# A state-space block on one core: the table request moved into the scan, two thirds of a convolution moved to VectorE, y sums one slot earlier, decay weights made later

## The chip, the cores and the metric

The kernel runs on one core of a Trainium2 chip. A core has TensorE (PE: matmuls; its weight loads are counted apart as PEld), VectorE (DVE), ScalarE (ACT), GpSimd (POOL) and SyncE (SP), which here issues all the transfers. Each engine works through its own queue in order and waits on semaphores. The metric is the device time of one launch in microseconds (us), the median of several runs.

## The reference

The input x has 8 images of 96 channels with 64 x 64 pixels. Layer 0 is a group norm (groups of three channels) and a vision state-space block, with a residual. Layer 1 is an attention without softmax and a small feed-forward net in a coarse float format, both with residuals. What matters here is the block:

```
xh      = layernorm(groupnorm(x))
xi, z   = split(xh @ in_proj_w.T + in_proj_b)        # 192 channels each
xi      = silu(depthwise 3x3 conv(xi) + conv_b)
xs      = xi in 4 orders of its 4096 pixels          # rows, columns, both reversed
dts,B,C = xs @ x_proj_w                              # per order
delta   = softplus(dts @ dt_proj_w + bias)
h[t]    = exp(delta[t] * A) * h[t-1] + delta[t] * xs[t] * B[t]   # 16 states per channel
y[t]    = sum over states of h[t] * C[t]  +  D * xs[t]
out     = x + (layernorm(sum of the 4 y) * silu(z)) @ out_proj_w.T + b
```

A is -exp(A_log), a constant. Every sum is in fp32, but for the feed-forward net.

## The kernel before, in words

The images are worked off in four pairs, each through five stages.

**front** (L217) normalizes both images chunk by chunk (8 chunks of 512 pixels; L261 to L270), projects them (L276 to L303) and convolves. The projected channels lie in three padded images `ybuf`: T = 0 and 1 hold channels 0 to 127 of the first and second image, T = 2 the last 64 of both (64 partitions each). The depthwise convolution is nine matmuls per chunk with a diagonal weight matrix `diag` (L311), added up in PSUM; ACT applies Silu on the way out into `xi[T]` (L316). The diagonals are made by DVE at the start of each front, 18 of them (L226).

**prepare** (L329) makes delta, delta times input, B and C from `xi` and writes them to device memory in the layout of the scan. It ends with a request for the table set `LOGEXP`, in which ACT has both logarithm and exponential (L397). ACT evaluates a function only with a table set that contains it; where the set in force lacks the function, the compiler puts in a load.

**scan** (L400) goes over 4 orders x 32 time chunks = 128 steps. A step has eight slots v. In slot v, for p = 8s + v: PE multiplies delta by A for slot p + 2 and ACT takes exp in place (`decay`, L533 and L537); POOL makes delta u B for two slots at a time (`drive`, L515); DVE runs the recurrence over 774 columns (`run`, L548) from `da[p % 3]` and `dbu` into `h`; and PE sums the states of the step before with C as the weights (`sums`, L566), two of the sixteen positions of each block per group f, eight groups in all. After the groups 3 and 7 ACT takes the sums out of PSUM (`yev`, L574). `da` has three buffers, `dbu` three, `h` two. So the first `run` of step s + 1 writes the buffer of h that the groups of step s - 1 read, and these are worked off during step s. This part is written in a hand-made order (`manual_schedule`): each engine takes the instructions as the program has them.

**back** (L628) adds up the four orders through PE, normalizes (ln and exp, L698 and L699), gates and projects. **tail** (L717) does layer 1: a first part with a norm and the key and value products per chunk, a second with the feed-forward net; `norm` has a logarithm at L735 and an exponential at L736.

Outside the scan a planner orders the instructions on each engine: it simulates the program with costs of its own, takes what is ready, and prefers what comes first in the program. Pools that are closed give their space to pools opened after them, and a tile waits until the tiles that had its space have been read.

Before all this, constants are loaded, and the weights that multiply delta by A are made: exp of A_log, three bf16 parts of it, written to device memory (`ad`), read back spread over partitions, multiplied with a mask by DVE (`awp`, L179) and written out again (`awd`, 1.5 MB for each of the four orders). The scan loads them at L429, first at its own start.

Of the kernel before, what the change touches and what calls it, by code (L numbers as in the profile page):

```python
# [10 lines left out]
F32 = mybir.dt.float32  # L11
F16 = mybir.dt.float16
BF16 = mybir.dt.bfloat16
F8 = mybir.dt.float8e5
AF = mybir.ActivationFunctionType
ALU = mybir.AluOpType
# [4 lines left out]
DI = 192  # L21
NS = 16
RK = 6
KD = 4
HH = 64
L = HH * HH
F = 512
NCH = L // F
ROWS = F // HH
# [9 lines left out]
NE = 24  # L39
X0 = F - 3 * SEG  # L40
LOGEXP = "natural_log_exp_and_others"
# [10 lines left out]
def vss_attn_ffn(ctx: ExitStack, tc: tile.TileContext, a: dict):  # L52
    nc = tc.nc
# [13 lines left out]
    ident = const.tile([128, 128], F32, name="ident")  # L67
# [13 lines left out]
    for e in range(4):  # L81
        rows = slice(NE * e, NE * e + NE)
# [9 lines left out]
    convw = load("convw", [128, 2, 9])  # L92
    convb = load("convb", [128, 2])
# [5 lines left out]
    with tc.tile_pool(name="xprep", bufs=2) as wp:  # L99
        for k in range(KD):  # L100
            for g in range(2):
                xg = wp.tile([128, 3, 2 * NS], F32, name="xg")
                nc.sync.dma_start(xg, a["xw"][k, :, g, :, 0:32])
                for b in range(2):
                    o = 32 * g + NS * b
# [31 lines left out]
    for g in range(2):  # L137
        for e in range(4):
# [1 line left out]
                dpad[:, g, 32 * e : 32 * e + NE], ident[0:DIM, NE * e : NE * e + NE],  # L140
                dsum[:, g : g + 1], None, ALU.mult,
            )

    ad = dram.tile([3, KD, DI, NS], BF16, name="ad", bufs=1)
    awd = dram.tile([KD, 128, 48 * 128], BF16, name="awd", bufs=1)
    with tc.tile_pool(name="aprep", bufs=1) as wp:
        am = wp.tile([128, KD, 2, NS], F32, name="am")  # L150
        nc.sync.dma_start(am, a["alog"])
        nc.scalar.activation(am, am, AF.Exp)
        nc.vector.tensor_scalar(am, am, -1.0, None, ALU.mult)
        for i in range(3):
            ap = wp.tile([128, KD, 2, NS], BF16, name=f"ap{i}")
            nc.vector.tensor_copy(ap, am)
            if i < 2:
                nc.vector.tensor_tensor(am, am, ap, ALU.subtract)
            for k in range(KD):
                nc.sync.dma_start(ad[i, k, 0:128], ap[:, k, 0])  # L160
                nc.sync.dma_start(ad[i, k, 128:DI], ap[0:64, k, 1])
        mask = wp.tile([128, 16], F32, name="mask")
        for p in range(3):
            nc.sync.dma_start(
                mask[32 * p : 32 * p + 32],
                ident[0:16, 0:16].unsqueeze(1).to_broadcast([16, 2, 16]),
            )
        for p in range(2):
            nc.sync.dma_start(mask[96 + 16 * p : 112 + 16 * p], ident[0:16, 0:16])
        for k in range(KD):  # L170
            ac = wp.tile([128, NE * NS], BF16, name="ac", bufs=2)
            for i, rows, n in ((0, slice(0, 96, 2), 6), (1, slice(1, 96, 2), 6), (2, slice(96, 128), 4)):
                nc.sync.dma_start(
                    ac[rows],
                    ad[i, k].rearrange("(s c) n -> s (c n)", s=8).unsqueeze(0)
                    .to_broadcast([n, 8, NE * NS]),
                )
            aw = wp.tile([128, 48, 16, 8], BF16, name="awp", bufs=2)
            nc.vector.tensor_tensor(  # L179
                aw,  # L180
                ac.rearrange("p (c n) -> p c n", n=8).unsqueeze(2).to_broadcast([128, 48, 16, 8]),
                mask.unsqueeze(1).unsqueeze(3).to_broadcast([128, 48, 16, 8]), ALU.mult,
            )
            nc.sync.dma_start(awd[k], aw.rearrange("p c m n -> p (c m n)"))


    blk = const.tile([128, 16], F32, name="blk")
    nc.sync.dma_start(blk, ident[0:16, 0:16].unsqueeze(1).to_broadcast([16, 8, 16]))
# [24 lines left out]
    def half(T):  # L213
        return 1 if T == 2 else 0


    def front(pair, xi, zs, ybuf):  # L217
        with ExitStack() as st:
            p1 = st.enter_context(tc.tile_pool(name="p1", bufs=1))
            tmp = st.enter_context(tc.tile_pool(name="p1t", bufs=2))  # L220
            ps = st.enter_context(tc.tile_pool(name="p1ps", bufs=4, space=PSUM))

            diag = p1.tile([128, 2, 9, 128], F32, name="diag")
            for j in range(2):
                for t in range(9):
                    nc.vector.tensor_scalar(  # L226
                        diag[:, j, t, :], ident, convw[:, j, t : t + 1], None, ALU.mult
                    )
            pad = [t.rearrange("p (h w) -> p h w", w=HH + 2) for t in ybuf]
            for t in ybuf:  # L230
                nc.gpsimd.memset(t, 0.0)
# [38 lines left out]
                    nc.vector.tensor_scalar(xt[:, cs], xt[:, cs], nw, nb, ALU.mult, ALU.add)  # L270


            for b in range(2):
                xt = xts[b]
                lo = slice(64 * b, 64 * b + 64)
                for c in range(NCH):  # L276
                    cs = bass.ts(c, F)
                    r0 = c * ROWS
                    pm = ps.tile([128, F], F32, name="pm", tag="ps")
                    nc.tensor.matmul(pm, winT[:, 0:128], xt[:, cs], start=True, stop=True)  # L280
                    pl = ps.tile([128, F], F32, name="pl", tag="ps")
                    nc.tensor.matmul(pl[lo], winT[:, 128:DI], xt[:, cs], start=True, stop=True)
                    nc.scalar.activation(
                        pad[b][:, r0 + 1 : r0 + 1 + ROWS, 1 : HH + 1],
                        pm.rearrange("p (h w) -> p h w", w=HH),
                        AF.Identity, bias=inb[:, 0:1],
                    )
                    nc.scalar.activation(
                        pad[2][lo, r0 + 1 : r0 + 1 + ROWS, 1 : HH + 1],
                        pl[lo].rearrange("p (h w) -> p h w", w=HH),  # L290
                        AF.Identity, bias=inb[lo, 1:2],
                    )
                    zt = tmp.tile([DIM, 2, F], F32, name="zt")
                    for g in range(2):
                        pz = ps.tile([128, F], F32, name="pz", tag="ps")
                        nc.tensor.matmul(
                            pz[:DIM], winT[:, DI + g * DIM : DI + (g + 1) * DIM], xt[:, cs],
                            start=True, stop=True,
                        )
                        nc.scalar.activation(  # L300
                            zt[:, g], pz[:DIM], AF.Silu, bias=inz[:, g]
                        )
                    nc.sync.dma_start(zs[b, :, :, cs].rearrange("g p l -> p g l"), zt)  # L303

            for T in range(3):
                for c in range(NCH):
                    r0 = c * ROWS
                    pc = ps.tile([128, F], F32, name="pc", tag="ps")
                    for t in range(9):
                        dy, dx = divmod(t, 3)  # L310
                        nc.tensor.matmul(  # L311
                            pc, diag[:, half(T), t, :],
                            pad[T][:, r0 + dy : r0 + dy + ROWS, dx : dx + HH],
                            start=(t == 0), stop=(t == 8),
                        )
                    nc.scalar.activation(  # L316
                        xi[T][:, bass.ts(c, F)], pc, AF.Silu, bias=convb[:, half(T) : half(T) + 1]
                    )

    def spread(dst, T, src):  # L320

# [7 lines left out]
    def prepare(xi, us, dl, du, bs, cs_):  # L329
        with ExitStack() as st:  # L330
# [8 lines left out]
            for o in range(2):  # L339
                for c in range(NCH):  # L340
# [12 lines left out]
                    for k in (o, o + 2):  # L353
# [12 lines left out]
                        for T in range(3):  # L366
# [27 lines left out]
                                .rearrange("j a p t -> p (j a) t"),  # L394
                                T, dp.rearrange("p j a t -> p (j a) t"),
                            )
            nc.scalar.preload_act_table_set(LOGEXP)  # L397


    def scan(dl, du, bs, cs_, ys):  # L400
        with ExitStack() as st:
            st.enter_context(tc.manual_schedule())
            one = st.enter_context(tc.tile_pool(name="s1", bufs=1))
            wk = st.enter_context(tc.tile_pool(name="s2", bufs=2))
            trio = st.enter_context(tc.tile_pool(name="s3", bufs=3))
# [196 lines left out]
            for s in range(N + 2):  # L602
                for v in range(8):
                    p = 8 * s + v
                    if s < N:
                        decay(p + 2)
                        if v % 2 == 0:
                            drive(p // 2 + 2)
                        run(p)
                    if 0 < s <= N:  # L610
                        sums(s - 1, v)
                    if s < N:
                        if v == 0:
                            load(s + 1)
                        if v == 1:
                            fetch(2 * s + 3)
                        if v == 5:
                            fetch(2 * s + 4)
                        if s + 1 < N and steps[s + 1][2] and v % 2 == 1:
                            load_aw(steps[s + 1][0], v // 2)  # L620
                    if v == 3 and s > 1:
                        store(s - 2)
                    if v == 0:
                        more = diagonal(s + 1) if s % NB else load_bc(s + NB)
                    next(more, None)
# [197 lines left out]
    for pair in range(npair):  # L823
# [7 lines left out]
        with tc.tile_pool(name="xip", bufs=1) as xp:  # L831
            xi = [xp.tile([128, L], F32, name=f"xi{T}") for T in range(3)]
            with tc.tile_pool(name="yp", bufs=1) as yp:

                ybuf = [yp.tile([128, (HH + 2) ** 2], F32, name=f"y{T}") for T in range(3)]
                front(pair, xi, zs, ybuf)
            prepare(xi, us, dl, du, bs, cs_)
        scan(dl, du, bs, cs_, ys)
        with tc.tile_pool(name="t1p", bufs=1) as tp:
# [117 lines left out]
```

## Time and profile before

| | |
|---|---|
| time, median of 3 runs | 13196.79 us (13184.92 to 13217.89) |
| profiled execution | 13189.4 us |
| PE busy | 9569.7 us (73%) |
| DVE busy | 8359.3 us (63%) |
| POOL busy | 7825.5 us (59%) |
| ACT busy | 7498.9 us (57%) |
| DMA | 2043.74 MB, 155 GB/s over the span |

The stages of the second pair, by the first and last instruction of their lines in the trace: norm of the front from 3374.9 us, projection from 3465, convolution 3529.5 to 3715, preparation to about 4057, scan to 5970, back end to 6280, tail to about 6615. The busy shares are means over these stages. A group of instructions has its line, engine, operation, output and inputs, count, busy time, the mean of one in ns, and the idle time of its engine just before it with what ended most of that. "issue" as a releaser means that the engine waited for nothing that the profile shows.

### The profile page before, as it was taken

What the parts mean: (1) busy time and instruction counts of PE and PEld (TensorE: products, weight loads), DVE (VectorE), ACT (ScalarE), POOL (GpSimd) and SP (SyncE); (2) the same over time, 40 slices, a digit from 0 to 9 for tenths busy, and PEclk for the clock granted to TensorE, in tenths of its full rate; (3) what the DMA queues carried; (4) which work ended last, traced back from release to release, by engine and by line L of the source; (5) the groups of instructions that cost most, each with busy time, mean ns of one, the idle gap of its engine ahead of it and who ended that gap; (6) DMA issues with size and microseconds to landing.
All of it is one profiled execution on the core that took longest, in us unless ns stands there. A gap on an engine that the chain in (4) does not pass through costs nothing. (4 is left out here: it accounts for less than half of the span.)

```text
span 13189.4 us, 405730 instructions
## 1 busy us (share of the span) xinstructions
PE 9569.7 (73%) x179456; PEld 6167.3 (47%) x179456; DVE 8359.3 (63%) x6293; ACT 7498.9 (57%) x12586; POOL 7825.5 (59%) x2686
## 2 busy tenths in 40 slices
PE   7966666687796666668779566666868956666686
PEld 2245555553224555555322455555533245555553
DVE  2378988932137999992213799899221389999822
ACT  2456666635445666663544666666254566666625
POOL 0379999910037999990003799999000389999900
PEclk9778888896777888889677788888967688888896
DMA  2788888861178888886017888888601888888860
GB/s 60 158 198 197 198 196 199 197 139 23 38 160 200 198 199 204 200 200 138 9 37 178 199 202 196 197 202 196 128 11 41 177 201 200 197 200 202 188 127 10
DMA packets 1627316, 2043.74 MB, mean 155 GB/s; under 512 B 958083, under 2 KB 1303252, under 8 KB 1622740
## 3 DMA queue, kind: packets, MB, share of 16 engines
q1 hardware_dynamic: 1625556, 2017.78, 66.8%
q8 instruction: 1408, 23.07, 0.8%
q14 instruction: 352, 2.88, 0.1%
HBM read 1579.00 MB, written 438.38 MB: 153 GB/s over the span
## 5 line engine op out<-in xcount | busy, mean ns | idle before, releaser
L515 POOL TENSOR_TENSOR dbu<-dut,bc 128x1536 f32<-128x1536 f32 x2048 | 7083.1, 3506 | 602.9 <-ACT dbu L512 516.2
L548 DVE TENSOR_TENSOR_SCAN h<-da,dbu 128x774 f32<-128x774 f32 x4096 | 6973.8, 1756 | 732.9 <-ACT da L537 419.2
L537 ACT ACTIVATE da<-da 128x768 f32<-128x768 f32 x4096 | 3263.9, 797 | 2210.4 <-PE da L533 2161.8
L566 PE MATMUL yp<-h,cw 128*32 128x48 f32 x131072 | 3172.0, 242 | 925.7 <-issue 911.4
L533 PE MATMUL da<-dm,aw 128*128 128x128 bf16 x24576 | 2424.9, 244 | 1736.8 <-DVE h L548 1384.4
L566 PEld LDWEIGHTS yp<-h,cw 128*32 128x32 f32 x131072 | 2534.7, 153 | 1519.2 <-issue 1191.2
L533 PEld LDWEIGHTS <-aw 128*128 128x128 bf16 x24576 | 1825.1, 108 | 1994.5 <-issue 1649.4
L469 ACT ACTIVATE cw<-bc,blk 128x512 f32<-128x512 f32 x2048 | 1478.3, 723 | 268.0 <-DMA bc<-cs 240.4
L348 POOL COPY u<-xi 128x512 f32<-128x512 f32 x96 | 110.1, 1160 | 1517.7 <-PE pc L311 1486.8
L391 POOL TENSOR_TENSOR dp<-rest,dp 128x512 bf16<-128x512 f32 x384 | 458.4, 1194 | 713.6 <-ACT dp L390 701.2
L742 POOL MEMSET tn<- 1x4096 f32 x8 | 27.8, 3506 | 1311.4 <-DVE t L712 1311.4
L376 DVE TENSOR_TENSOR du<-delta,xi 128x512 f32<-128x512 f32 x192 | 133.0, 692 | 1060.9 <-ACT delta L372 772.5
L812 POOL TENSOR_TENSOR ot<-t,y 96x512 f32<-96x512 f32 x64 | 73.5, 1148 | 1176.2 <-DVE y L810 1150.2
L311 PE MATMUL pc<-y,diag 128*128 128x512 f32 x1728 | 742.3, 592 | 0.0
L389 DVE TENSOR_TENSOR rest<-delta,dp 128x512 f32<-128x512 f32 x384 | 303.9, 792 | 662.7 <-ACT dp L388 662.7
L368 PE MATMUL pq<-S,dtw 12*128 12x512 f32 x768 | 582.2, 866 | 122.7 <-ACT delta L372 75.3
L574 ACT ACTIVATE yev<-yp 128x384 f32<-128x384 f32 x1024 | 500.0, 488 | 198.5 <-PE yp L566 185.4
L674 PEld LDWEIGHTS py<-ident,yk 128*24 128x24 f32 x16384 | 449.3, 103 | 177.9 <-issue 176.6
L674 PE MATMUL py<-ident,yk 128*24 128x128 f32 x16384 | 509.8, 275 | 23.9 <-issue 23.5
L311 PEld LDWEIGHTS pc<-y,diag 128*128 128x128 f32 x1728 | 326.4, 189 | 415.4 <-issue 415.4
L316 ACT ACTIVATE xi<-pc,c_convb 128x512 f32<-128x512 f32 x96 | 66.0, 687 | 675.8 <-PE pc L311 675.8
L681 ACT ACTIVATE yt<-py 128x512 f32<-128x512 f32 x64 | 38.2, 597 | 721.0 <-PE py L674 670.7
(133 smaller groups left out, 7591.7 us busy)
## 6 DMA issues: line engine op xcount, KB each, us to landing
dut<-du SPq DMA_DIRECT2D x1024, 768.0 KB
dm<-dl SPq DMA_DIRECT2D x512, 576.0 KB
dl<-dp SPq DMA_DIRECT2D x256, 384.0 KB
dm<-dl SPq DMA_DIRECT2D x512, 192.0 KB
ys<-yev SPq DMA_DIRECT2D x1024, 96.0 KB
du<-du SPq DMA_DIRECT2D x256, 256.0 KB
bc<-bs SPq DMA_DIRECT2D x512, 128.0 KB
bc<-cs SPq DMA_DIRECT2D x512, 128.0 KB
```

The costliest lines, as they stand in the source:

```text
L311: nc.tensor.matmul(pc, diag[:, half(T), t, :], pad[T][:, r0 + dy : r0 + dy + ROWS, dx : dx + HH], start=(t == 0), stop=(t == 8),)
L368: nc.tensor.matmul(pq, dtw[64:76, k, T], S[64:76], start=True, stop=True)
L389: nc.vector.tensor_tensor(rest, d, dp[:, :, 0], ALU.subtract)
L391: nc.gpsimd.tensor_tensor(dp[:, :, 2], rest, dp[:, :, 1], ALU.subtract)
L469: nc.scalar.activation(cw[i % 2][:, :, :, m, :].rearrange("p z j t -> p (z j) t"), bc[i][:, 1].rearrange("p z (j t) -> p (z j) t", j=NB), ...
L515: nc.gpsimd.tensor_tensor(segs(t)[:, :, :, 1:], dut[g // 2][:, NI * (r % 2) : NI * (r % 2) + NI, :].unsqueeze(1) .to_broadcast([128, 2, NI ...
L533: nc.tensor.matmul(e[:, i], aw[k, r][:, i, z, :], dm[s][:, NI * r + i, :], start=True, stop=True,)
L537: nc.scalar.activation(e, e, AF.Exp)
L548: nc.vector.tensor_tensor_scan(hs[s][:, w, r][:, d], da[p % 3][:, o : o + W6][:, d], dbu[4 * s + r][:, w][:, d], 0.0, ALU.mult, ALU.add,)
L566: nc.tensor.matmul(y[32 * q : 32 * q + 32, 2 * NE * i : 2 * NE * i + 2 * NE] .rearrange("p (j r i) -> p i j r", j=2, r=NR), w[:, z, :, t], ...
L574: nc.scalar.activation(yev[s][:, :, o : o + 8, :].rearrange("p j i e -> p i j e"), y[:, 0 : 16 * NE].rearrange("p (i j e) -> p i j e", j=2 ...
L674: nc.tensor.matmul(o, yk[:, k, 4 * g + e, NE * j : NE * j + NE], ident, start=False, stop=(k + j == KD + 2),)
```

## The change

Four edits, each for a reason of its own:

- **Table request.** The request for `LOGEXP` leaves the end of `prepare`, where the planner places it, and becomes the first instruction of `scan`, where the written order holds.
- **Convolution.** Only T = 1 stays on PE. T = 0 and T = 2 become nine multiply-add passes on DVE over whole images (`taps`), with Silu in place on ACT behind them. T = 0 is traced after the projection of the first image, T = 2 after both. `diag` keeps nine diagonals.
- **y sums.** The groups 0 and 1 go into slot 0, each later group into one slot earlier, and slot 7 has none. This is meant to free the buffer of h before the next step needs it.
- **Weights for delta A.** The code becomes a function, called once, behind the front of the first pair, so that the constants' way to the first pair is shorter.

```
-    with tc.tile_pool(name="aprep", bufs=1) as wp:
...
+    def decay_weights():
+        with tc.tile_pool(name="aprep", bufs=1) as wp:
...
...
-            diag = p1.tile([128, 2, 9, 128], F32, name="diag")
-            for j in range(2):
-                for t in range(9):
-                    nc.vector.tensor_scalar(
-                        diag[:, j, t, :], ident, convw[:, j, t : t + 1], None, ALU.mult
-                    )
+            diag = p1.tile([128, 9, 128], F32, name="diag")
+            for t in range(9):
+                nc.vector.tensor_scalar(
+                    diag[:, t, :], ident, convw[:, 0, t : t + 1], None, ALU.mult
+                )
...
+            def taps(T):
+                for t in range(9):
+                    dy, dx = divmod(t, 3)
+                    w = convw[:, half(T), t : t + 1]
+                    v = pad[T][:, dy : dy + HH, dx : dx + HH]
+                    o = xi[T].rearrange("p (h w) -> p h w", w=HH)
+                    if t == 0:
+                        nc.vector.tensor_scalar(o, v, w, None, ALU.mult)
+                    else:
+                        nc.vector.scalar_tensor_tensor(o, v, w, o, ALU.mult, ALU.add)
+                for c in range(NCH):
+                    xc = xi[T][:, bass.ts(c, F)]
+                    nc.scalar.activation(
+                        xc, xc, AF.Silu, bias=convb[:, half(T) : half(T) + 1]
+                    )
...
+                if b == 0:
+                    taps(0)
+            taps(2)
-            for T in range(3):
-                for c in range(NCH):
+            for c in range(NCH):
...
-            nc.scalar.preload_act_table_set(LOGEXP)       # end of prepare
...
             st.enter_context(tc.manual_schedule())        # start of scan
+            nc.scalar.preload_act_table_set(LOGEXP)
...
                     if 0 < s <= N:
-                        sums(s - 1, v)
+                        for f in ((0, 1), (2,), (3,), (4,), (5,), (6,), (7,), ())[v]:
+                            sums(s - 1, f)
...
                 front(pair, xi, zs, ybuf)
+            if pair == 0:
+                decay_weights()
             prepare(xi, us, dl, du, bs, cs_)
```

## Prediction

> **What bounds the kernel now.** I read the table of time by stage first. It gives span, PE, weight loads, DVE, ACT and POOL busy (with counts), granted clock, DMA share and GB/s; the second pair of images is shown, stage by stage.
>
> ```profile
> 3380.00:3470.00 90.00, 60.87 (x69) 16.00 (x68) 23.29 (x38) 72.00 (x85) 0.00 (x0) 0.50 0.00 0
> 3470.00:3530.00 60.00, 60.00 (x126) 18.45 (x125) 0.00 (x0) 43.31 (x63) 0.00 (x0) 0.97 0.33 99
> 3530.00:3715.00 185.00, 185.00 (x432) 81.13 (x430) 0.00 (x0) 16.16 (x24) 0.00 (x0) 1.00 0.06 25
> 3834.00:4057.00 223.00, 157.94 (x213) 40.23 (x212) 105.00 (x130) 118.19 (x203) 102.47 (x83) 0.64 0.96 214
> 4057.00:5966.00 1909.00, 1291.27 (x38554) 1080.81 (x38555) 1737.56 (x1021) 1276.89 (x2285) 1770.58 (x527) 0.86 0.85 198
> 5966.00:6280.00 314.00, 275.24 (x4761) 165.83 (x4761) 68.56 (x95) 87.86 (x111) 1.39 (x1) 0.97 0.68 134
> 6280.00:6420.00 140.00, 100.97 (x346) 65.36 (x345) 17.19 (x30) 90.11 (x118) 6.95 (x2) 0.78 0.00 1
> ```
>
> These are layer norm, input projection, convolution, preparation, scan, back end and the first part of the tail. Each has another limit. The convolution is PE alone: 185 of 185 us, and DVE does nothing. Preparation is full of DMA (0.96). The scan is DVE and POOL together.
>
> Next, groups by line (busy, mean ns of one, idle before and who ended it), then what the scan instruction waited for in the first pair (us, times), then ACT's groups that load a table.
>
> ```profile
> L316 ACT ACTIVATE xi<-pc,c_convb 128x512 f32<-128x512 f32 x96 | 66.0, 687 | 675.8 <-PE pc L311 675.8
> L548 DVE TENSOR_TENSOR_SCAN h<-da,dbu 128x774 f32<-128x774 f32 x4096 | 6973.8, 1756 | 732.9 <-ACT da L537 419.2
> ```
>
> ```profile
>   ACT da L537: 116.4, 64
>   PE yp L566: 66.3, 39
>   POOL dbu L515: 6.9, 33
> ```
>
> ```profile
> L735 ACT ACT_TABLE_LOAD x128 | 164.2, 1283 | 2.3
> L736 ACT ACT_TABLE_LOAD x128 | 164.2, 1283 | 2.3
> L698 ACT ACT_TABLE_LOAD x64 | 82.1, 1283 | 1.2
> L699 ACT ACT_TABLE_LOAD x64 | 82.1, 1283 | 1.2
> L267 ACT ACT_TABLE_LOAD x48 | 61.6, 1283 | 0.9
> L268 ACT ACT_TABLE_LOAD x48 | 61.6, 1283 | 0.9
> L537 ACT ACT_TABLE_LOAD x4 | 5.1, 1283 | 0.1
> ```
>
> The reader is to see three things. The convolution's ACT waits 675.8 us for PE. The scan's 1756 ns x 1024 = 1798 us per pair are a floor, and of the idle time above it 66 us ends with the y sums on PE. And every logarithm and every exponential of back end and tail loads a table. The old request at L397 appears nowhere in the trace, while L537, the scan's exponential, loads a set itself in each pair: the request has no effect today.
>
> **What the Trainium skill says.** *ScalarE: Activation LUTs*, "Table sets: the hidden batching unit": one set holds both functions, so ln then exp needs one load. The trace agrees: L267 and L268 run 16 times each in the first pair with no load (48, not 64), after the request at L66. The same page, "What ACT_TABLE_LOAD costs", gives 1283 ns plus a drain of 1380. The trace shows 1283, but the exponential begins 0.01 us behind it, so I take 1.28 us. *VectorE: DVE Perf Modes*, "The perf-mode tier table": fp32 tensor_scalar reaches 2x, tensor_tensor 1x. The trace agrees for the first (4096 elements in 2.40 us, L256); it has no row for scalar_tensor_tensor.
>
> **Convolution.** Today 24 chunks at 7.725 us (start to start of the ACT rows at L316) = 185 us. Halves T = 0 and 2 leave PE; T = 1 keeps 8 x 7.725 = 62 us. One tap on DVE, from L706 (512 elements, all in SBUF, 740 ns) and 1 cycle an element: about 740 + 3584 x 1.04 ns = 4.5 us. Nine taps: eight at 4.5 plus a first at 2.4 to 4.5, so 38 to 40 us per half. Lower bound, if these ops ran at the 2x of L256: 22 us; upper, if the rows of 64 break the stream: 55. I take 40. Projection of the first image ends some 32 us after the stage's start, of the second 61 us. Half 0 then runs on DVE from 32 to 72, half 2 from 72 to 112, its eight Silu passes (0.69 us) to 118. The PE convolution runs from 61 to 123 and still ends last, by 5 us; it hides both halves. Gain 123 us a pair. What is queued behind the new wait: the Silu of half 0 stands in ACT's queue near the evacuations of the second image's projection, and if it is placed too early, those and PE wait for DVE. I deduct 5 us a pair for that: 118 x 4 = 472 us. Preparation begins earlier as a whole; its DMA limit moves with it.
>
> **The diagonals** halve from 18 to 9. From the second pair on they stand before the statistics in DVE's order (14.35 us for 18), so 7.2 x 3 = 22 us.
>
> **Table request.** Put in the scan's own hand-ordered program it is fixed ahead of the exponential, which is in the set; square, copy, ln and exp of back end, tail and the next front then load nothing, until Silu. Removed: 440 loads in L735/736, L698/699 and L267/268, plus 12 in L254/255, together 580 us of ACT. On the path is less: the load before ln mostly lies beside the matmul that ln waits for; the one before exp does not.
> - Norm in the front: 5.22 us a chunk in pairs 2 to 4 against 4.41 in the first. 0.81 x 16 x 3 = 39, plus about 9 for the single statistics: 48 us.
> - Last part of the tail: a period of 12.14 us in which PE waits 2.15 us for tq; 1.3 x 16 x 4 = 83 us.
> - First part: 14 us per round with four loads, ACT 91 of 140 us, PE 101. PE becomes the limit at 12 us or so: 2.3 x 8 x 4 = 75 us.
> - Back end: 18.09 us per round, PE waits 1.25 us for g; 1.23 x 16 x 4 = 79 us.
> Sum 285 us (180 to 350).
>
> **y sums one slot ahead.** Slot 0 gets two groups, slot 7 none. Today the last group stands behind decay matmuls that wait for the scan of slot 6, and h has two buffers, so the first scan of the next step waits for it. The wait of 66 us (67, 53, 52 in the others) should go. Most of it comes from PE pauses of 2.5 to 4.7 us with no releaser in the trace ("issue"), about one in 30 us. Those remain, but with the group 1.75 us earlier and decay two scans ahead, a 2.6 us pause is hidden and a 3.5 us one costs about 1.5 us. I let 70% of 238 us go: 170 us (60 to 240). The double slot adds 0.7 us to PE before the next decay, which has about 1.7 us to spare (3.5 us of lookahead less 0.5 us matmuls, 0.8 us exp and two handovers). POOL, 3.505 us per two scans, is as fast as DVE and not the limit.
>
> **Weights for delta A.** At the front of the first pair they hold the load of x until 53 us, and four DVE products of 6.5 us stand among the statistics: normalization starts at 83.7 us. Without them x is asked for near 33 us, behind the constants that the queue has issued by 30; 12 us to arrive (53.4 to 65.1 today), 5 for eight statistics, 4 for the small steps: about 54, so 30 us are won. Behind the front they take space that the padded inputs had and that preparation's tiles take next, so preparation waits for their chain: two products after the convolution's end, each with a 1.5 MB store behind it, about 30 us. I take 0, with -30 to +35.
>
> **Sum.** 472 + 22 + 285 + 170 + 0 = 949; 13197 - 949 = **12,250 us**.
>
> **Rivals.**
> - *The request is void again.* For: it was so at L397, and nothing shows why. Against: at L66 it worked, and the scan keeps its written order. 12,250 + 285 = 12,535.
> - *DVE becomes the front's bound.* Taps of 6 us, or ACT's queue held by them, halve the gain: 12,250 + 236 = 12,486. For: half 2 ends only 5 us before PE.
> - *The scan wins nothing:* each PE pause moves to "ACT da", already 419 us in all. 12,420.
> - *Slower.* The double slot puts 0.7 us on the path of each of 512 steps (358 us), DVE takes as long as PE did, the request is void: 13,197 + 358 - 22 = 13,533. Against: PE waits for DVE 0.5 to 0.7 us in nearly every slot, so it has the room.
>
> **How the numbers follow.** Forecast 0.60, void request 0.10, DVE bound 0.14, scan nothing 0.12, slower 0.04. The best ends of all terms give about 12,060; the first and second rival end at 12,535 and 12,486. Range 12,040 to 12,540. Faster 0.95, same 0.01, slower 0.04.
>
> **What would show it.** PE convolution time per pair 62 us with DVE at 80 us beside it; no table loads at L735/736 and their like; "PE yp" gone from the scan's waits and scan spans near 1,865 us; normalization starting near 54 us in the first pair. Wrong it would be if taps took over 5 us each, if ACT waits for them inside the projection, if loads stay, or if "ACT da" grows by what "PE yp" loses.

## The result, and the profile after

The changed kernel takes **12690.28 us** (median of 4 runs, 12684.31 to 12694.4), against 13197.52 for the kernel before (4 runs). The ratio is 0.9614 (95% interval 0.9597 to 0.9631): 507 us are won. The forecast was 12,250, so 440 us of the expected 949 are missing. A time below that stands without a ratio is that of one launch.

First the table of time by stage, for the second pair: stretch, its length, then PE, weight loads, DVE, ACT, POOL busy (with counts), granted clock, DMA share, GB/s. The rows are norm, projection, convolution, preparation, scan.

```profile
3241.60:3333.00 91.40, 61.53 (x69) 16.65 (x70) 26.17 (x43) 71.02 (x82) 0.00 (x0) 0.50 0.00 0
3333.00:3396.00 63.00, 63.00 (x129) 18.88 (x128) 26.93 (x9) 46.33 (x67) 0.00 (x0) 0.94 0.32 94
3396.00:3458.00 62.00, 61.95 (x145) 26.98 (x143) 50.23 (x12) 15.31 (x25) 0.00 (x0) 1.00 0.18 57
3458.00:3829.00 371.00, 288.58 (x402) 75.08 (x403) 149.40 (x198) 196.87 (x333) 157.11 (x127) 0.64 0.91 204
3829.20:5735.30 1906.10, 1309.66 (x38638) 1092.90 (x38637) 1754.38 (x1024) 1258.56 (x2277) 1764.25 (x523) 0.82 0.85 197
```

The convolution is 62 us instead of 185, and still PE's: 61.95 of 62. DVE works through projection and convolution, 27 and 50 us, and the convolution still ends with PE. The norm (91 us; 90 before) and the scan (1906; 1909) are as they were.

Next, groups by line: ACT's Silu behind the PE convolution, DVE's taps, DVE's scan.

```profile
L335 ACT ACTIVATE xi<-pc,c_convb 128x512 f32<-128x512 f32 x32 | 21.9, 685 | 173.2 <-PE pc L331 173.2
...
L283 DVE SCALAR_TENSOR_TENSOR xi<-y,c_convw,xi 128x4096 f32<-128x4096 f32 x64 | 285.2, 4482 | 1.4
...
L565 DVE TENSOR_TENSOR_SCAN h<-da,dbu 128x774 f32<-128x774 f32 x4096 | 7027.2, 1760 | 641.5 <-ACT da L554 503.2 <-PE yp L583 39.3 <-ACT dbu L529 31.6
```

Then what the scan instruction waited for in the first pair (us, times).

```profile
  ACT da L554: 125.1, 65
  PE yp L583: 9.5, 5
  ACT dbu L529: 8.0, 9
  POOL dbu L532: 3.7, 20
```

The wait on the y sums is nearly gone, 66 to 9.5 us, and the wait on delta A has grown by 9. Over all pairs "PE yp" falls from 239 to 39 us, in these lines of before and after, and "ACT da" rises from 419 to 503.

```profile
  PE yp L566: 238.6, 158
...
  PE yp L583: 39.3, 21
```

The scan's idle time falls from 733 only to 642, and of these 91 us only 37 come off the span of the scans: the busy time of the scan instructions has grown by 53, from 6973.8 to 7027.2 us. Why it has grown is open.

Last, ACT's table loads.

```profile
L753 ACT ACT_TABLE_LOAD x128 | 164.2, 1283 | 2.3
...
L716 ACT ACT_TABLE_LOAD x64 | 82.1, 1283 | 1.1
...
L267 ACT ACT_TABLE_LOAD x48 | 61.6, 1283 | 0.8
...
L554 ACT ACT_TABLE_LOAD x4 | 5.1, 1283 | 0.1
```

They are the loads of before, and one more in the setup. The request, now at L419, appears nowhere, and the scan's exponential at L554 still loads a set in each pair.

The profiled executions (13189.4 and 12691.4 us, 498 apart) give this balance, by the first and last starts of each stage's instructions:

| stage | won, us |
|---|---|
| convolution, 4 x (186.3 - 62.7) | 494 |
| first pair until its convolution (237.5 to 200.0) | 37 |
| preparation of the first pair (356.6 to 409.5) | -53 |
| preparation of the others (356.5, 357, 364.5 to 370.5, 355.2, 368.1) | -16 |
| scans (1919.7, 1897.3, 1903.8, 1908.3 to 1896.8, 1906.1, 1893.6, 1895.1) | 37 |
| sum | 499 |

Back end, tail and norm together changed by about 1 us. The other edits and the scatter of the stages sum to nearly nothing: the time is that of the convolution alone. Small terms are not to be trusted to the last microsecond. Over the traces of this case the later preparations take 351 to 378 us and the projections 64 to 79, whatever the kernel, so the -16, and 7 of the 37 before the first convolution, may be chance.

### The profile page after: what moved, and what is told of

It reads as the page before. It is cut to its first block, busy times and chain, and to the rows that moved or that the text cites. A ratio compares the mean times of both kernels' runs of the same rounds, so it can differ in the third digit from the quotient of the medians.

```text
span 12691.4 us, 403490 instructions
## 1 busy us (share of the span) xinstructions
PE 9112.9 (72%) x178304; PEld 5967.4 (47%) x178304; DVE 8711.4 (69%) x6329; ACT 7451.3 (59%) x12587; POOL 7833.1 (62%) x2686
## 3 DMA queue, kind: packets, MB, share of 16 engines
q8 instruction: 1399, 22.92, 0.9%
## 5 line engine op out<-in xcount | busy, mean ns | idle before, releaser
L565 DVE TENSOR_TENSOR_SCAN h<-da,dbu 128x774 f32<-128x774 f32 x4096 | 7027.2, 1760 | 641.5 <-ACT da L554 503.2
L554 ACT ACTIVATE da<-da 128x768 f32<-128x768 f32 x4096 | 3258.1, 798 | 2132.6 <-PE da L550 2098.6
L583 PE MATMUL yp<-h,cw 128*32 128x48 f32 x131072 | 3127.9, 245 | 1059.9 <-issue 1045.2
L550 PE MATMUL da<-dm,aw 128*128 128x128 bf16 x24576 | 2486.4, 250 | 1534.3 <-DVE h L565 1162.5
L721 DVE SCALAR_TENSOR_TENSOR g<-yc,c_onw,yrs 96x512 f32<-96x512 f32 x128 | 89.9, 742 | 556.6 <-ACT yrs L717 556.6
L385 PEld LDWEIGHTS pq<-S,dtw 12*128 12x128 f32 x768 | 160.4, 250 | 610.8 <-ACT delta L389 176.0
L407 ACT ACTIVATE dp<-rest 128x512 bf16<-128x512 f32 x384 | 241.4, 630 | 326.4 <-DVE rest L406 326.4
L529 ACT COPY dbu<-h 128x12 f32<-128x12 f32 x1984 | 407.7, 205 | 0.0
```

What stands on the lines that cost most here:

```text
L385: nc.tensor.matmul(pq, dtw[64:76, k, T], S[64:76], start=True, stop=True)
L529: nc.scalar.copy(start, segs(hs[s - 1][:, :, r])[:, :, :, 1 if back else TC])
L550: nc.tensor.matmul(e[:, i], aw[k, r][:, i, z, :], dm[s][:, NI * r + i, :], start=True, stop=True,)
L554: nc.scalar.activation(e, e, AF.Exp)
L565: nc.vector.tensor_tensor_scan(hs[s][:, w, r][:, d], da[p % 3][:, o : o + W6][:, d], dbu[4 * s + r][:, w][:, d], 0.0, ALU.mult, ALU.add,)
L583: nc.tensor.matmul(y[32 * q : 32 * q + 32, 2 * NE * i : 2 * NE * i + 2 * NE] .rearrange("p (j r i) -> p i j r", j=2, r=NR), w[:, z, :, t], ...
```

## The experiments

The theory after the result had three parts: the convolution's gain is all there is; the request is void because something replaces its set before the scan's exponential; and the y sums won little because PE's pauses without releaser hit another wait. The rival to the first was that several small gains had been cancelled by as many losses.

### Each edit undone

**convolution_on_PE** takes the changed kernel and puts 18 diagonals and three PE halves back, with the order of before:

```
-            diag = p1.tile([128, 9, 128], F32, name="diag")
+            diag = p1.tile([128, 2, 9, 128], F32, name="diag")
...
-                if b == 0:
-                    taps(0)
-            taps(2)
-            for c in range(NCH):
+            for T in range(3):
+                for c in range(NCH):
```

> The changed kernel with all three convolutions on PE again, in the old place. Theory: each pair loses the 123.6 us that the trace shows, 494 us in all: about 13,184 us. Rival: the preparation behind it is bound by DMA, which gives part of it back: under 13,080 us.

Measured: 13218.28 us, ratio to the kernel before 1.0007 (0.9995 to 1.002). With the other three edits and without this one there is no gain left that can be measured. The edit is worth 528 us by the medians, 494 by the trace. The theory's 13,184 was 34 us too low; the rival's bound of 13,080 is far off.

**sums_as_before** puts each group of y sums back into its own slot:

```
-                        for f in ((0, 1), (2,), (3,), (4,), (5,), (6,), (7,), ())[v]:
-                            sums(s - 1, f)
+                        sums(s - 1, v)
```

> The changed kernel with the y sums in their old slots. Theory: the edit traded the wait for the sums for a wait for the decay, and is worth some 37 us (the sum of the four scan spans): about 12,727 us. The forecast's size, 170 us, would give 12,860 us. Rival: the double slot costs as much as the early end brings: 12,690 us.

Measured: 12751.13 us, ratio 0.9669 (0.9638 to 0.97). The edit is worth 61 us by the medians and 50 by the spans of the scans (7642 against 7592 us), above the theory's 37 and far below the forecast's 170. The scan again waits for "PE yp", 273 us, and less for "ACT da", 410: the two waits trade places. The size stays rough, since one trace a kernel is little: convolution_on_PE has the early sums too, and its scans add up to 7641 us, as many as here.

**weights_at_the_front** makes the weights for delta A before the first front again. It is not the old place: there they stood ahead of the constants of the feed-forward net, here behind them.

```
+    decay_weights()
+
     def front(pair, xi, zs, ybuf):
...
-            if pair == 0:
-                decay_weights()
```

> The changed kernel with the weights for delta A made ahead of the first front again. Theory: behind the front they win 30 us of start and lose 53 us at the head of the first preparation, whose first copy waits 52.3 us for the last store; undone, the time falls by 23 us to about 12,667 us. The forecast had 0: 12,690 us. Rival: the start's 30 us count and the wait was hidden: 12,720 us.

Measured: 12665.75 us, ratio 0.9601 (0.9566 to 0.9636). By the medians the move costs 24 us, as expected; the interval overlaps that of the changed kernel, so the time alone does not settle it. The way there was not the expected one. In this trace x is asked for at 33.8 us and normalization starts at 54.7, as in the changed kernel (33.5 and 53.4), so the early start isn't lost here; the norm of the first pair takes 89 us instead of 75, the first preparation 356 instead of 410, and the first scan starts at 634.8 us instead of 672.3. So the old place, ahead of those constants, was not tried again, and what the move brought is known from the balance alone. The waits in the first preparation of the changed kernel show the cost directly (who waited for whom: us in total, times, longest).

```profile
POOL u L365 <- DMA awd<-awp: 305.6, 1, 305.6
...
ACT S L377 <- DMA awd<-awp: 52.3, 1, 52.3
```

Preparation's first tile `S` lies where the weights lay and waits 52 us until they are written out. (POOL's 305 us are mostly time in which it had nothing to do.) That is the 53 us by which the first preparation grew; the earlier start gives back 37.

### Where the request goes

**pin_request** leaves everything but the place of the request. It goes from the head of the scan's program behind the first of the ACT copies of C, which waits for data:

```
-            nc.scalar.preload_act_table_set(LOGEXP)
             one = st.enter_context(tc.tile_pool(name="s1", bufs=1))
...
-            for _ in diagonal(0):
+            todo = diagonal(0)
+            next(todo)
+            nc.scalar.preload_act_table_set(LOGEXP)
+            for _ in todo:
                 pass
```

> The changed kernel with the table request behind the first copy that builds C's weights in the scan, instead of at the scan's head. Theory: at the head the request waits for nothing, so the planner sets it ahead of the preparation's last Softplus, whose own load replaces it; behind an instruction that waits it stays. Then the 456 loads before ln, exp and the statistics go, 14 loads are left, and the time falls by the 285 us of the forecast, to about 12,405 us. Rival 1: a request inside the scan is dropped wherever it stands: loads as they are, 12,690 us. Rival 2: the loads go, but they lay beside other work: loads gone and over 12,600 us.

Measured: **12344.37 us**, ratio 0.935 (0.9307 to 0.9393), 346 us under the changed kernel. ACT's table loads are now these, and two single ones in the setup.

```profile
L317 ACT ACT_TABLE_LOAD x4 | 5.1, 1283 | 0.1
L389 ACT ACT_TABLE_LOAD x4 | 5.1, 1283 | 0.1
L612 ACT ACT_TABLE_LOAD x4 | 5.1, 1283 | 0.0
```

L317 and L389 are Silu and Softplus, L612 is the request: for the first time it stands in the trace, once per pair, and 492 loads have gone. From the last scan instruction of a pair to the first matmul of the next norm it is now 593.4, 594.1 and 596.5 us instead of 672.5, 679.6 and 677.0, and from the last scan instruction of all to the end 570 instead of 645. The norms of the later pairs take 74.6 us instead of 89.6. In sum 245 + 75 + 3 x 15 = 365 us, a little more than the medians give. (The four launches lie between 12,279 and 12,376 us, and the profiled one was the fastest.) The size in the forecast (285) was low; the mechanism holds as soon as the request stays.

The reading of why it did not stay: the written order holds among the scan's own instructions. A request at their head waits for nothing, so nothing keeps it behind preparation's Softplus at L389, whose own load then replaces the set. Behind a copy that waits for the scan's first data it can't go ahead. The traces show both ends of this (no load and no effect in one place, four loads and full effect in the other); a request that was passed over leaves no record, so the step between, who set it ahead and when, is inferred.

### What holds the scan

In the trace of the changed kernel, PE stops between matmuls of one group. This is the timeline: start, length, instruction, and in brackets the idle time before it and who ended it.

```profile
4263.44 0.39 PE L583 MATMUL yp<-h,cw 128*32 128x48 f32 x6 [2.52 <-issue]
...
4263.76 0.83 PE L550 MATMUL da<-dm,aw 128*128 128x128 bf16 x6
...
4264.62 0.80 ACT L554 ACTIVATE da<-da 128x768 f32<-128x768 f32 x1 [3.02 <-PE da L550]
...
4265.52 1.77 DVE L565 TENSOR_TENSOR_SCAN h<-da,dbu 128x774 f32<-128x774 f32 x1 [2.10 <-ACT da L554]
```

PE idles 2.52 us for no reason in the profile, six matmuls before the end of a group. The matmuls of delta A come behind it, then the exponential, and the scan loses 2.10 us. With the sums one slot ahead the pause no longer delays the buffer of h, but it still delays the next `decay`, which has only the 1.7 us to spare that the prediction worked out. Between 4300 and 5020 us there are 41 such pauses over 1 us, 104 us in all. The line of the y sums has the total, 1045 us of "issue" ahead of them:

```profile
L583 PE MATMUL yp<-h,cw 128*32 128x48 f32 x131072 | 3127.9, 245 | 1059.9 <-issue 1045.2
```

How much of "ACT da" comes from there can be counted in the trace. Of its 503 us, 368 come right behind such a pause (the exponential waits for PE, and a pause over 0.5 us ended at most 2.5 us before), and 118 behind a copy of C that holds ACT because its load is late.

**double_group_late** asks whether the double slot costs something where it stands. It moves it to slot 6:

```
-                        for f in ((0, 1), (2,), (3,), (4,), (5,), (6,), (7,), ())[v]:
+                        for f in ((0,), (1,), (2,), (3,), (4,), (5,), (6, 7), ())[v]:
```

> The changed kernel with the two groups together in slot 6 instead of slot 0; slot 7 stays empty. Theory (pauses set the waits, not the double slot): the time stays at 12,690 us within 20. Rival (the double slot in front of the next decay is what makes it late): at least 60 us away from it, down if slot 0 was the wrong place.

Measured: 12742.59 us, ratio 0.9654 (0.9615 to 0.9694), 52 us above the changed kernel, more than the theory's 20 and less than the rival's 60; the intervals overlap. "PE yp" returns to 178 us and "ACT da" stays at 473. The early double slot isn't the brake: moved away from the head of the step, it brings nothing.

**no_delta_loads** leaves out all but three of a scan's 256 loads of delta u, so that most products use old data:

```
+                if g > 2:
+                    dut[g] = dut[g % 3]
+                    return
```

> The changed kernel with delta u loaded three times per scan instead of 256 times; the products use the old data, so this leaves out the loads and the right values. Some 390 of the scan's 470 MB per pair on the transfer engines' reading side go with it. Theory: PE's pauses without a releaser are late instructions, held up by the data transfers; with these thinned out PE's idle before the y sums (issue) falls from about 240 us per pair to under 80, the wait of the recurrence for the decay from 126 to under 50 us, and the scan from 1,897 to about 1,825 us. Rival: the double slot makes the decay late by itself; the wait stays above 100 us and the scan near 1,890 us.

Measured: 12177.48 us. The share of these loads was put too high in that text: by the page they are 796 of 2044 MB. The scans take 1770 us each instead of 1893 to 1906, and DVE idles 138 us in all. PE's time on "issue" ahead of the y sums falls from 1045 to 3.4 us. **no_delta_loads_sums_as_before** is the same with the y sums in their old slots.

> As the run before, with the same loads left out, and the y sums in their old slots. Theory: without pauses the waits for the sums shrink to the few tenths of a us per step that the order itself costs, 128 x 0.3 = 38 us per pair, so this scan is 30 to 40 us longer than that of the run before. Rival: the edit pays only by hiding pauses; both scans are alike within 10 us.

Measured: 12175.91 us, scans of 1769 us. Its rival holds: without pauses the order of the sums is worth nothing (1770 and 1769 us a scan), so what the edit won was the hiding of pauses.

Two more kernels separate the traffic from the number of loads. Both issue every load of delta u and cut its length beyond the third (`w` of twelve rows, 1 or 6):

```
-                dut[g] = trio.tile([128, 2 * NI, TC], F32, name="dut")
+                w = 1 if g > 2 else 2 * NI
+                dut[g] = dut[g % 3] if g > 2 else one.tile([128, 2 * NI, TC], F32, name=f"dut{g}")
...
-                    dut[g].rearrange("p i t -> p (i t)"),
+                    dut[g][:, 0:w].rearrange("p i t -> p (i t)"),
...
```

> All loads of delta u are issued, but all beyond the third of a scan fetch one of twelve rows (64 instead of 768 KB); the rest of their product is left wrong. Theory (the traffic delays PE's instructions): as with the loads left out: issue ahead of the y sums under 30 us, scans near 1775 us each, 12,170 to 12,220 us. Rival (it is the issuing of 256 loads per scan and the waits on them that holds PE back): issue stays over 700 us and the time over 12,500.

> The same with six of twelve rows (384 KB per load), so DMA share in the scan near 0.6. Theory (queueing behind data): pauses fall more than in proportion, issue 100 to 450 us, scans 1790 to 1840 us each, 12,230 to 12,450 us. Rival (a threshold, pauses come only when the DMA engines are full): issue under 50 us and 12,180 to 12,200. A second rival, pauses in proportion to bytes: issue over 500 us.

Measured: **short_delta_loads** 12175.27 us, issue 2.5 us, scans of 1770 us. So it is not the issuing of the loads, nor the waits on them. **half_delta_loads** 12198.91 us, with scans of 1770 to 1771 us. Its groups of PE and DVE, by line:

```profile
L584 PE MATMUL yp<-h,cw 128*32 128x48 f32 x131072 | 2875.6, 237 | 39.8 <-issue 26.5
...
L566 DVE TENSOR_TENSOR_SCAN h<-da,dbu 128x774 f32<-128x774 f32 x4096 | 7021.5, 1758 | 138.1 <-ACT da L555 70.5
```

And a stretch of scan in the first pair, first of the changed kernel, then of this one; granted clock, DMA share and GB/s are the last three numbers.

```profile
1000.00:2400.00 1400.00, 948.64 (x28466) 793.05 (x28466) 1286.49 (x751) 925.94 (x1676) 1297.51 (x388) 0.85 0.86 199
...
1000.00:2400.00 1400.00, 954.15 (x30672) 822.83 (x30671) 1385.53 (x809) 1009.14 (x1809) 1399.04 (x417) 0.92 0.58 158
```

At a DMA share of 0.58 nothing is left of the pauses (26.5 us of issue), at 0.86 they are at 1045. My theory of a gradual fall missed: the effect is steep, nearer to the rival with a threshold.

**half_the_y_sums** keeps all transfers and leaves out half of the y sums:

```
-                    for z in range(2):
+                    for z in range(1):
...
-                                start=(i + z == 0), stop=(i + z == 8),
+                                start=(i == 0), stop=(i == 7),
```

> Leaves out half of the y sums (the second half of the columns of h is not summed), all transfers stay. PE's instructions per step fall from 352 to 224 (matmuls and weight loads). Theory (the pauses are late PE instructions, fetched over the same DMA engines as the data): pauses come per instruction, so the 'issue' time ahead of the y sums falls from 1045 us to about 650 or less, although the DMA share stays near 0.86, and the scans become shorter by at least 150 us in all. Rival (pauses come with time, from full transfers, whatever PE is asked to do): issue stays at 900 to 1050 us, and the scans lose what little ends with PE yp, under 60 us.

Measured: 12478.44 us; the scans take 1847 to 1862 us, 173 less in sum than in the changed kernel. There is not one PE pause over 1 us without releaser between 4300 and 5020 us, where the changed kernel has 41, although the DMA share is 0.88 there, as in the same stretch of the first pair:

```profile
1000.00:2400.00 1400.00, 971.44 (x16944) 761.20 (x16944) 1315.88 (x772) 946.15 (x1726) 1323.83 (x398) 0.51 0.88 204
```

So the pauses come with the number of PE's instructions and with the traffic, both. The page says what joins them. Its DMA queues in the changed kernel (packets, MB, share of 16 engines):

```profile
q1 hardware_dynamic: 1625556, 2017.78, 69.4%
q8 instruction: 1399, 22.92, 0.9%
```

And in half_the_y_sums:

```profile
q8 instruction: 887, 14.53, 0.6%
```

Queue 8 carries PE's instructions, and it moves 22.92 MB / 1399 = 16.4 KB at a time. Half of the sums are 65,536 matmuls and as many weight loads fewer, and 512 packets fewer: 131,072 / 512 = 256 instructions in each. The Trainium skill describes this on *Runtime: NRT & Kernel Launch*, "Instruction fetch mechanics": a sequencer fetches its instructions with a DMA queue of its own, in blocks of 16 KiB, 256 instructions. It calls the cost mostly hidden. Here that is so in the kernels with thinned loads and not in this one. I counted PE's matmuls and weight loads from each of the 41 pauses to the next; six of the 40 distances, with the time at which the last packet of queue 8 before the pause's end had landed:

```
pause ends   packet landed   next after   instructions   / 256
4326.2       4324.7          21.8 us       767           3.00
4348.0       4346.6           9.4 us       252           0.98
4357.4       4356.1          17.3 us       767           3.00
4374.8       4373.3          14.2 us       508           1.98
4420.5       4418.9          29.4 us      1275           4.98
4478.1       4476.6          51.8 us      2297           8.97
```

All 40 distances are within 0.03 of a whole number of blocks. With PE's semaphore instructions counted too, all 40 are exact multiples of 256, and in the four scans together 455 of 457. Every pause stands at the edge of a block. The packets of queue 8 are in the trace one by one, and they show the rest. Each of the 461 pauses over 1 us in the scans ends 1.2 to 2.1 us behind the landing of a 16 KB packet; for the pause of 4263.44 above it is 4261.91. Such a packet takes 1.3 us (1.1 without the loads of delta u), so it isn't slow, it starts late: behind the moment when PE entered the block before, by 2.8 us in the median and up to 7.2 in the changed kernel, by 1.0 with half loads and 0.65 without. A block lasts 6.3 us here. So PE has no more than one block ahead, and where the next fetch starts late PE runs out of instructions. What it waits for before it starts no record names; that it is the transfers of the data follows from the runs with thinned loads.

The same run shows a **second** way in which the traffic holds the scan. With the pauses gone, DVE still idles 501 us, 488 of them on "ACT da". The timeline of half_the_y_sums at one of these:

```profile
4308.76 0.72 ACT L486 ACTIVATE cw<-bc,blk 128x512 f32<-128x512 f32 x1 [5.00 <-DMA bc<-cs]
4309.39 0.79 ACT L554 ACTIVATE da<-da 128x768 f32<-128x768 f32 x1
...
4310.21 3.43 DVE L565 TENSOR_TENSOR_SCAN h<-da,dbu 128x774 f32<-128x774 f32 x2 [3.07 <-ACT da L554]
```

The exponential had its matmuls some 3 us before; it stood in ACT's queue behind a copy of C that waited 5 us for its load. That is the rule in this run: 423 of the 488 us follow such a copy, and only 47 an exponential that waited for PE, although the clock granted to PE was low (0.61 over the run, 0.80 in the changed kernel). The waits of these copies are 902 us in this run, 212 in the changed kernel and 52 with half loads. Take one consequence of full DMA engines away and the other grows.

### The best version

**request_pinned_own_space** is pin_request with a place in memory of its own for the weights' tiles, opened ahead of the first pair's pools, so that preparation doesn't inherit it:

```
+        with ExitStack() as own:
+            if pair == 0:
+                wp = own.enter_context(tc.tile_pool(name="aprep", bufs=1))
+            xp = own.enter_context(tc.tile_pool(name="xip", bufs=1))
...
-                decay_weights()
+                decay_weights(wp)
```

> The changed kernel with the request pinned as before, and the pool of the weights for delta A opened ahead of the first pair's big tiles, so that neither the front's nor the preparation's tiles share its space. Theory: the 52 us at the head of the first preparation go, all else stays: 12,344 less 52 is about 12,292 us. Rival: the transfers of the weights (6 MB) then lie in the preparation, which is bound by DMA, and cost 30 us there: 12,322 us or more.

Measured: **12280.49 us**, ratio 0.9305 (0.9278 to 0.9331), 64 us under pin_request by the medians and 410 under the changed kernel. The intervals of the two pinned kernels overlap, and the traces show less than 64: the first preparation is 47 us shorter (365.2 instead of 412.2), but the products for the weights now lie in the first norm, which is 17 us longer, and the first scan instruction starts at 637.7 us instead of 668.0. So 30 us are shown, between the theory's 52 and the rival's 22. This is what the change was after, with the request and the weights' tiles in other places.

## Why the prediction was wrong, step by step

- **Convolution: right.** Forecast 123 us a pair gross, measured 123.6. One tap takes 4.48 us (forecast 4.5); against the 0.74 us for 512 elements at L706 that is 3.74 us for 3584 more, 1.04 ns an element, as the forecast had it. PE still ends last, 6.5 us behind the last Silu of the taps. The 5 us a pair deducted for a Silu that holds ACT weren't needed: ACT waited once, 3.2 us, in the second pair. Forecast 472, measured 494.
- **Diagonals: too high.** 22 us were expected; the norm stage of the second pair is no shorter. Nine of them take 12.58 us there where 18 took 14.35: POOL clears the padded images at the same time.

```profile
3216.45 12.58 DVE L226 TENSOR_SCALAR diag<-ident,c_convw 128x128 f32<-128x128 f32 x9 [3.56 <-DMA out_dram<-ot]
3216.46 11.07 POOL L231 MEMSET y<- 128x4356 f32 x3 [2.28 <-issue]
```

  Seven of the nine take about 0.27 us; the first two end together, 0.1 us behind POOL's last memset, after 11.15 and 11.02 us. Of the 18 before it was two as well. So halving their number takes away only short ones. The Trainium skill, *GPSIMD Engine Reference*, "Specifications", says that POOL's interfaces to SBUF are shared with VectorE and that there is contention with its instructions in a 2-port mode; the trace fits that reading, but no run here took the memset away.
- **Table request: the step that failed.** "Put in the scan's own hand-ordered program it is fixed ahead of the exponential, which is in the set" is wrong for this place. It brought 0 instead of 285 us. A place behind a waiting instruction brings 346 (pin_request), so the gain had been worked out too low, by its back end and tail: about 80 us a pair instead of 59. (The forecast also counted 452 loads that would go; 492 went.) The forecast had the warning in its own view, since the old request at L397 was void too, and gave it a chance of 0.10 because "the scan keeps its written order". That order says nothing of the instructions ahead of the scan.
- **y sums: the second, in size.** 170 us expected, 37 in the trace, 50 to 61 by undoing it, with the scatter named there. The wait "PE yp" did go, from 239 to 39 us, more than the 70% assumed. But "a 2.6 us pause is hidden" holds only for the buffer of h; the same pause delays `decay` in the same queue, and "ACT da" took 84 us over. The rival *the scan wins nothing* named this. What neither had is the cause: PE's instructions arrive late, and the order of the sums only moves the wait. Nor was 1798 us a floor for a scan: the instructions overlap in the trace (6973.8 / 4 = 1743 us of busy time a pair), and with thinned loads a scan takes 1770.
- **Weights: too optimistic by some 20 us.** Start and cost were named rightly, about 30 us won at the start of the norm (53.4 instead of 83.7; forecast 54). Preparation's wait is 52 us, not 30. The trace gives -16, inside the bounds of -30 to +35; the run, whose place is a third one, -24.

Put together: 494 + 0 + 0 + 37 - 16 - 16 for later preparation = 499 against the 498 of the profiles; 285 for the request and 133 for the sums make up 418 of the 440 us missing. The rival *request is void again* had 12,535; with the sums at 37 it would have been 12,668, within 22 us of the result. The nearness of the convolution's term is no luck: its time and its overlap are in the trace as they were forecast. That this rival comes so near is partly luck: the convolution brought 22 us more than forecast, while diagonals, weights and later preparation fell short by 22, 16 and 16.

## What to carry to other kernels

Do not take it that a request which waits for nothing is held by the order written around it; in two places here it had no effect. Tie it behind an instruction that waits for the data of its stage, and look for its own line in the trace. When an engine idles with "issue" as the releaser in the middle of a group, count instructions between such gaps; at multiples of 256 suspect late instruction blocks, and look whether each gap ends just behind a packet of the instruction queue. Fewer bytes on the DMA engines or fewer instructions on that engine helped here where reordering didn't. A wait that vanishes from the list is no gain until the span of the stage has fallen with it: here the wait fell by 199 us, the idle time by 91 and the scans by 37.

## What the runs showed of the hardware that was not expected

- Instruction blocks contend with data. At a DMA share of 0.86 in the scan PE loses 1045 us to "issue" ahead of the y sums, at 0.58 26.5 us, at 0.41 2.5 us. In the stretch counted, 104 of 720 us were pauses at block edges.
- A block that lasts 1.7 times as long hides it: in half_the_y_sums no pause over 1 us is left between 4300 and 5020 us at a share of 0.88. PE's records count 352 instructions a step there and 608 in the changed kernel (each fp32 matmul of the program and its weight load stand twice in the trace; the expectation's 224 and 352 had them once). So a block lasts 10.5 instead of 6.2 us (256 / 352 of 1855 / 128 us, and 256 / 608 of 1898 / 128 us), and the packets of queue 8 come every 10.4 and 6.3 us.
- PE has no more than one block of instructions ahead: in the median the next fetch starts 2.8 us behind PE's entry into the block before, and lands 1.3 us later.
- A tensor_scalar of DVE that meets a memset of POOL can last as long as the memset: 11.15 us instead of 0.27.
- An exponential begins 0.01 us behind its 1283 ns table load, so 1.28 us a load is the price on ACT. On the path it was less: 492 loads are 631 us, and 346 to 365 were won.
